# Four-layer convolution net on one core: where layer 1's first kernel is finished, relative to the first input transform

## The chip, the cores and the metric

The kernel runs on one core of a Trainium2 chip. The metric is device time in microseconds (us), median of several runs; smaller is better. Engines are called by the profile's names: PE (TensorE, matmul), PEld (its weight loads), DVE (VectorE), ACT (ScalarE), POOL (GpSimd), SP (SyncE, which issues most DMAs; ACT issues the others). A name such as L296 is line 296 of the kernel before.

## The reference

The input is `x` of 3 images, 256 channels, 48 by 48 pixels, in float32. Four residual layers follow each other:

```
x = x + L0(_gn(x))   # 1x1 conv + two rounds of attention and MLP + 1x1 conv over the concatenation
x = x + L1(_gn(x))   # per-image 3x3 convolution, kernel mixed from 8 experts
x = x + L2(_gn(x))   # one 3x3 convolution with bias
x = x + L3(_gn(x))   # a state-space scan over the pixels
```

`_gn` is a group normalisation over 32 groups of channels. Layer 1 is where the change lies:

```
pooled  = x.mean(axis=(2, 3))
routing = sigmoid(pooled @ routing_ws)                 # one weight per image and expert
ws      = einsum('ne,eoihw->noihw', routing, weight)   # a 3x3 kernel of its own for each image
y       = 3x3 convolution of image n with ws[n], padding 1
```

So no convolution of an image can begin before its own kernel has been mixed: 8 experts of 256 x 256 x 9 weights, each times that image's weight.

## The kernel before

**The end of layer 0.** The images are taken in `ORDER = (2, 1, 0)`; the loop variable `n` counts 0, 1, 2 and `b` is the image. For each image the last MLP runs over six chunks ("strips") `c` of 384 columns: `hidden` (L518 matmuls, L523 gelu on ACT), then `add_back` of the strip before (L529 matmuls, L533 on DVE). Then the concatenating 1x1 convolution runs over the same six strips: `concatenated` (L1031 matmuls, L1036 SiLU on ACT, L1041 the residual addition on POOL). `take_stats` (L1045, DVE) collects the statistics of the strip before. The strips' operands `yc` and `xc` are loaded on ACT's DMA queue (L1020, L1022).

**What is slipped in beside it.** After each strip `aside` is called. It takes one step of a short generator (`small_steps`) and then a given number of steps of the generator `mixing`, which is `mixed(2, upools[0])`: the kernel of image 2.

- `routing(b)` is the short generator for the weights of an image: group statistics (L183 to L192, with matmuls L186 and L195 and the power on POOL L164), scale and shift, `pooled`, and then the product. For each of the two channel halves, DVE spreads `pooled` over a 128x128 tile `pbc` (L373, one buffer), and PE multiplies it with the routing weights (L374). ACT takes the sigmoid (L378). It is stepped during the MLP of the next image; image 0 has no next one and its routing is run at once after the loop.
- `mixed` makes 48 steps, 8 experts times 6 pieces: each loads 384 KB from HBM on SP (L251, tile `wconv`, six buffers) and scales or adds it into the tile `u` (first expert on ACT, L294; the other 42 on DVE, L296). After those come two steps with a `kernel_transform` each, for one half of the input channels: six DVE operations on 128x768 (L258 to L263) that turn the three taps of a row into six Winograd points in `u`. These use `wconv` buffers for their intermediate sums.

**The first input transform.** At `b == 0 and c == 3` the kernel calls `input_transform(2, 0, ...)`: POOL zeroes the edges of `xpad` (L322, L325), ACT writes the normalised half image of image 2 (L331), and twelve DVE operations on 128x624 (L345 to L356) form six Winograd points in the tile `vt`. The third of them (L347) writes point 1, the fourth (L348) point 3. `xpad` has one buffer, `vt` two.

**Order.** From the mark before this loop up to the end of `mixing`, `keep_order` chains the instructions of PE, DVE, ACT and POOL in the order written. It doesn't chain SP's loads. What comes later, image 0's routing and all of layer 1, is placed by the framework's planner, which may put it between chained instructions.

**Layer 1.** Units go over images 2, 1, 0, two halves each, two output halves `m` each. `products` makes one Winograd point in six matmuls (L1589), in the order 1, 3, 4, 5, 0, 2; the sums go to DVE (L1607 to L1619). Beside unit 0 (image 2) the kernel of image 1 is mixed, beside unit 1 that of image 0, each with its transforms; one piece of the mixture in six is summed on PE (L282). From unit 2 on nothing is mixed any more.

Of the kernel before, what the change touches and what calls it, by code (L numbers as in the profile page):

```python
# [84 lines left out]
def net(  # L85
# [29 lines left out]
    def late_pool(name, bufs=1, stack=late_pools):  # L115
        return stack.enter_context(tc.tile_pool(name=name, bufs=bufs, side="right"))
# [93 lines left out]
    def group_norm_steps(b, psum, tag, stats=None, known=None):  # L210

        mv, gm, rstd = yield from norm_steps(
            [xs[b][:, ct, :] for ct in range(CT)], gmat, psum, tag, stats, known
        )
        sc = small.tile([P, CT], F32, name="gsc", bufs=4)
        nc.vector.tensor_copy(sc, rstd)
        sh = small.tile([P, CT], F32, name="gsh", bufs=4)
        nc.vector.scalar_tensor_tensor(sh, gm, -1.0, rstd, ALU.mult, ALU.mult)
        return mv, sc, sh
# [22 lines left out]
    def sixth(sc, sh):  # L242

        t = small.tile([P, 2, CT], F32, name="six", bufs=4)
        nc.vector.tensor_scalar(t[:, 0, :], sc, 1.0 / 6.0, None, ALU.mult)
        nc.vector.tensor_scalar(t[:, 1, :], sh, 1.0 / 6.0, None, ALU.mult)
        return t[:, 0, :], t[:, 1, :]
# [111 lines left out]
    def routing(b, psum, tag, stats):  # L359

        mv, sc, sh = yield from group_norm_steps(b, psum, tag, stats)
        norms[b] = sixth(sc, sh)
        pooled = small.tile([P, CT], F32, name="pooled")
        nc.vector.tensor_tensor(pooled, mv[:, :, 0], sc, ALU.mult)
        nc.vector.tensor_tensor(pooled, pooled, sh, ALU.add)
        yield
        pr = psum.tile([P, 512], F32, tag=tag, name="ps_r")  # L370
        for ct in range(CT):
            pbc = small.tile([P, P], F32, name="pbc", bufs=1)
            nc.vector.tensor_scalar(pbc, ones, pooled[:, ct : ct + 1], None, ALU.mult)  # L373
            nc.tensor.matmul(  # L374
                pr[:, :EXPERTS], pbc, rwt[:, ct, :], start=ct == 0, stop=ct == CT - 1
            )
        r = route[b] = const.tile([P, EXPERTS], F32, name=f"route{b}")
        nc.scalar.activation(r, pr[:, :EXPERTS], AF.Sigmoid)  # L378


    with ExitStack() as l0:
# [131 lines left out]
        def hidden(b, c):  # L513
            wf, fb = mlp[b]
            f = fpool.tile([P, 2, CH], F32, name="f")
            pf = pair()
            for m in range(2):
                nc.tensor.matmul(  # L518
                    pf[:, m, :CH], wf[:, m * P : (m + 1) * P], chunk(cur[b], c),
                    start=True, stop=True,  # L520
                )
            for m in range(2):
                nc.scalar.activation(f[:, m, :], pf[:, m, :CH], AF.Gelu, bias=fb[:, m : m + 1])  # L523
            return f

        def add_back(i, b, c, f):
            pf = psa.tile([P, 512], F32, name="acc")
            for m in range(2):
                nc.tensor.matmul(  # L529
                    pf[:, :CH], w("f2", (i * 2 + m) * P, P), f[:, m, :], start=m == 0, stop=m == 1  # L530
                )
            cc = chunk(cur[b], c)
            nc.vector.scalar_tensor_tensor(cc, pf[:, :CH], v("f2_b", i), cc, ALU.add, ALU.add)  # L533
# [483 lines left out]
        def parts(b, c):  # L1017

            yc = ypool.tile([P, 3, CH], F32, name="yc")
            nc.scalar.dma_start(yc, ycat[b][:, :, c * CH : (c + 1) * CH])  # L1020
            xc = ypool.tile([P, CT, CH], F32, name="xc")
            nc.scalar.dma_start(  # L1022
                xc, x[b, :, c * CH : (c + 1) * CH].rearrange("(t p) n -> p t n", p=P)
            )
            return yc, xc

        def concatenated(b, c, yc, xc):
            pz = pair()
            for m in range(2):
                for kt in range(4):  # L1030
                    nc.tensor.matmul(  # L1031
                        pz[:, m, :CH], w("cv2", kt * 256 + m * P, P),
                        yc[:, kt, :] if kt < 3 else chunk(cur[b], c), start=kt == 0, stop=kt == 3,
                    )
            for m in range(2):
                nc.scalar.activation(  # L1036
                    chunk(xs[b][:, m, :], c), pz[:, m, :CH], AF.Silu,
                    bias=b2sh[:, m : m + 1], scale=b2sc[:, m : m + 1],
                )
            both = xs[b][:, :, c * CH : (c + 1) * CH]  # L1040
            nc.gpsimd.tensor_tensor(both, both, xc, ALU.add)  # L1041

        def take_stats(b, c, stats):
            for m in range(2):
                nc.vector.bn_stats(stats[m][:, c, :], chunk(xs[b][:, m, :], c))  # L1045
# [8 lines left out]
        def aside(n):  # L1054

            if small_steps:
                try:
                    next(small_steps[0])
                except StopIteration:
                    del small_steps[0]  # L1060
            if 2 in route:
                for _ in range(n):
                    next(mixing, None)

        for n, b in enumerate(ORDER):
            held = None
            for c in range(NCH):
                f = hidden(b, c)
                if held is not None:
                    add_back(i, *held)  # L1070
                held = b, c, f
                aside(2)
            add_back(i, *held)
            stats = [
                small.tile([P, NCH, 6], F32, name=f"xst{m}", bufs=2) for m in range(CT)
            ]
            for c in range(NCH):
                concatenated(b, c, *ahead.pop(0))

                z = n * NCH + c + 2  # L1080
                if 3 <= z < len(chunks):
                    ahead.append(parts(*chunks[z]))
                if c:
                    take_stats(b, c - 1, stats)
                if b == 0 and c == 3:
                    vp = late_pool("vp", 2, last_pools)
                    pad = late_pool("pad", stack=last_pools)
                    first_v = input_transform(2, 0, *norms[2])
                aside(3)
            take_stats(b, NCH - 1, stats)  # L1090
            if b:
                curpools[b].close()
            small_steps.append(routing(b, psm, "m", stats))
# [485 lines left out]
    with ExitStack() as l1:  # L1579
# [117 lines left out]
        for n, (k, h) in enumerate(halves):  # L1697
            layer, b = units[k]
# [33 lines left out]
    with ExitStack() as l3:  # L1732
# [180 lines left out]
        for s, (at, m, h) in enumerate(steps):  # L1913
            if m == 0 and h == 1 and at + 2 <= last:
                fetch(at + 2)
            for part in range(8):
# [6 lines left out]
                if part == 0 and h == 0:  # L1923
                    c, n = (at, m + 1) if m + 1 < DI else (at + 1, 0)
# [69 lines left out]
def net_kernel(tc, *args):  # L1994

    with tc.tile_pool(name="flag", bufs=1) as pool:
        flag = pool.tile([1, 1], I32, name="flag")
        net(tc, *args, flag, False)
        bad = tc.nc.values_load(flag[:1, :1])
        with tc.If(bad > 0):  # L2000
            net(tc, *args, None, True)
# [77 lines left out]
```

## Time and profile before

| What | us |
|---|---|
| median of 3 runs | 3333.62 |
| lowest to highest of them | 3328.32 to 3335.85 |
| the profiled execution, device time | 3335.13 |
| its span in the profile | 3333.4 |
| PE busy | 3141.3 (94%) |
| DVE busy | 2862.1 (86%) |
| ACT busy | 2393.7 (72%) |
| POOL busy | 1334.0 (40%) |
| mean TensorE clock granted | 0.979 |

The span runs from the first to the last instruction of the profiled execution; 1.7 us lie around it. Times of places below are us from the span's start. Busy shares are averages over stages with different limits. The stage of the change lies at about 1440 to 1610 us, at the end of layer 0 and in the first unit of layer 1.

### The profile page before, as it was taken

Reading aid. Unit: us, or ns where it says so; the run is one execution under the profiler, and the core shown is the slowest. Engines: PE = TensorE matmul, PEld = TensorE weight load, DVE = VectorE, ACT = ScalarE, POOL = GpSimd, SP = SyncE. Lnnn points to the kernel's source line nnn. Section 1 sums busy time; section 2 is a strip of 40 time slices with the busy share of each in tenths; the row PEclk is TensorE's granted clock in tenths of the full one; section 3 lists DMA queues with packets and bytes.
Section 4 is the critical chain, followed back from the end, with each engine's and each line's share of the span. In section 5 each row is a group of like instructions: output and inputs, shape, how many; then the busy total and the mean of one; then the engine's idle time right before and its main releaser. Section 6 shows DMA issues by size and latency. Waiting matters only on the chain.

```text
span 3333.4 us, 54144 instructions
## 1 busy us (share of the span) xinstructions
PE 3141.3 (94%) x20890; PEld 1555.3 (47%) x20890; DVE 2862.1 (86%) x3234; ACT 2393.7 (72%) x3664; POOL 1334.0 (40%) x457
## 2 busy tenths in 40 slices
PE   7999999999999999988999997999999999999996
PEld 4334343353343434546777773444444444444442
DVE  3799989968988998369985448999999999999998
ACT  2688888838888887332323457888888888888884
POOL 0000000000000000120000007999999999999997
PEclk8999999999999999999999998999999999999997
DMA  4000000010000001475621025555555555455552
GB/s 167 32 8 10 8 8 7 8 47 5 8 7 8 10 8 44 162 248 200 204 75 41 34 65 138 133 128 131 135 135 141 134 139 135 122 134 139 146 131 56
DMA packets 182158, 290.76 MB, mean 87 GB/s; under 512 B 34737, under 2 KB 148465, under 8 KB 179970
## 3 DMA queue, kind: packets, MB, share of 16 engines
q1 hardware_dynamic: 168658, 267.15, 29.9%
q10 hardware_dynamic: 13232, 20.06, 1.8%
q8 instruction: 165, 2.70, 0.3%
q14 instruction: 103, 0.84, 0.1%
HBM read 236.24 MB, written 50.64 MB: 86 GB/s over the span
## 4 chain that ended last, share of the span: by engine, by line
PE 56%; DVE 29%; ACT 8%; issue 4%; DMA 3%; POOL 0%; SPq 0%; ACTq 0%; DVEq 0%; POOLq 0%
DVE hs L1860 20%; PE ps_s L638 16%; PE acc L651 14%; PE ps_c L1589 8%; DVE hs L1808 3%; ACT ps_da L1852 2%; PE ps_s L1031 2%; PE ps_y L462 2%; DVE u L296 2%; PE ps_m L665 2%; PE ps_m L711 1%; PE acc L529 1%; PE ps_s L518 1%; PE ps_g L1222 1%; DMA wconv<-in_we 1%
## 5 line engine op out<-in xcount | busy, mean ns | idle before, releaser
L642 ACT ACTIVATE pt<-ps_s 128x1024 f32<-128x1024 f32 x972 | 942.4, 1022 | 154.7 <-PE ps_s L638 142.1
L1860 DVE TENSOR_TENSOR_SCAN hs<-ps_da,hs 128x385 f32<-128x385 f32 x1152 | 1003.0, 940 | 5.8 <-ACT ps_da L1852 4.0
L857 DVE TENSOR_TENSOR part<-part,pt 128x2048 f32<-128x2048 f32 x396 | 906.8, 2290 | 41.2 <-ACT pt L642 18.4
L1852 ACT ACTIVATE ps_da<-dtr,u 128x384 f32<-128x384 f32 x1152 | 651.3, 580 | 119.9 <-DVE hs L1860 108.8
L164 POOL TENSOR_TENSOR rstd<-ve,mhalf 128x2 f32<-128x2 f32 (+1 forms) x26 | 16.3, 629 | 1475.1 <-DVE ve L162 1475.1
L638 PE MATMUL ps_s<-q,kt 32*128 32x512 f32 (+1 forms) x4320 | 576.3, 592 | 0.1
L651 PE MATMUL acc<-pt,vt 128*32 128x512 f32 (+1 forms) x4320 | 520.9, 561 | 0.2
L1589 PE MATMUL ps_c<-vt,u 128*128 128x288 f32 x1728 | 432.0, 411 | 21.6 <-DVE u L263 21.6
L1877 POOL TENSOR_TENSOR hc<-hs,x 128x3072 f32<-128x3072 f32 x72 | 405.3, 5629 | 11.5 <-DVE hs L1860 7.1
L1877 POOL TENSOR_TENSOR hc<-hs,bc 128x3072 f32<-128x3072 f32 x71 | 400.3, 5638 | 9.7 <-DVE hs L1860 5.5
L1589 PEld LDWEIGHTS ps_c<-vt,u 128*128 128x128 f32 x1728 | 330.4, 192 | 118.2 <-issue 20.4
L638 PEld LDWEIGHTS ps_s<-q,kt 32*128 32x128 f32 x4320 | 195.2, 183 | 199.1 <-issue 120.2
L651 PEld LDWEIGHTS acc<-pt,vt 128*32 128x32 f32 x4320 | 94.4, 108 | 353.4 <-issue 326.7
L1894 PE MATMUL ps_y<-hc,u 128*32 128x384 f32 x2304 | 227.3, 515 | 1.1 <-POOL hc L1877 1.1
L1273 PE MATMUL ps_g<-u 128*128 128x384 f32 x576 | 195.0, 491 | 23.3 <-ACT u L1269 23.3
L1826 POOL TENSOR_TENSOR hs<-dtur,x 128x1536 f32<-128x1536 f32 x72 | 209.2, 2905 | 7.3 <-DMA dtur<-dtud 7.3
L1826 POOL TENSOR_TENSOR hs<-dtur,bc 128x1536 f32<-128x1536 f32 x72 | 209.7, 2912 | 0.0
L1273 PEld LDWEIGHTS ps_g<-u 128*128 128x128 f32 x576 | 108.3, 190 | 106.9 <-ACT u L1269 34.5
L1605 ACT COPY cb<-ps_c 128x288 f32<-128x288 f32 x48 | 19.1, 398 | 155.8 <-PE ps_c L1589 141.4
L322 POOL MEMSET xpad<- 128x212 f32 x12 | 5.7, 471 | 308.2 <-ACT xpad L1640 229.1
L1894 PEld LDWEIGHTS ps_y<-hc,u 128*32 128x32 f32 x2304 | 62.1, 112 | 142.4 <-issue 129.6
L1392 PE MATMUL ps_g<-u 128*128 128x384 f32 x288 | 109.2, 513 | 13.0 <-ACT sz L1400 7.7
(275 smaller groups left out, 4137.7 us busy)
## 6 DMA issues: line engine op xcount, KB each, us to landing
wconv<-in_we SPq DMA_DIRECT2D x144, 384.0 KB, 4.2
dtr<-dtd SPq DMA_DIRECT2D x288, 192.0 KB, 3.7
dtur<-dtud SPq DMA_DIRECT2D x288, 96.0 KB, 4.2
wconv<-xd SPq DMA_DIRECT2D x36, 384.0 KB, 3.7
x<-bcd SPq DMA_DIRECT2D x72, 192.0 KB, 4.9
dtd<-x SPq DMA_DIRECT2D x36, 384.0 KB, 3.0
dtuq<-dtud SPq DMA_DIRECT2D x288, 48.0 KB, 2.0
bc<-bcd SPq DMA_DIRECT2D x72, 192.0 KB, 4.8
```

The source lines that it names most:

```text
L638: nc.tensor.matmul(s[:, j, cols], kt[r, mt * P : (mt + 1) * P], q[r, :n], start=True, stop=True,)
L642: nc.scalar.activation(p[:, h0 : h0 + 2, :], s, AF.Exp)
L651: nc.tensor.matmul(acc[h * HD : (h + 1) * HD, :n], vt[:, mt, g * P + h * HD : g * P + (h + 1) * HD], p[:, h, cols], start=mt == 0, stop=mt ...
L857: ): nc.vector.tensor_tensor(part, first, p, ALU.add)
L1273: nc.tensor.matmul(bank[m % 2], w3v["taps"][:, m, tap, :], w3v["xi"][:, m % 3, tap : tap + CH], start=tap == 0, stop=tap == DCONV - 1,)
L1392: nc.tensor.matmul(bank[j], w("in", ct * 512 + m * P, P), k.xn[:, ct, DCONV - 1 :], start=ct == 0, stop=ct == CT - 1,)
L1589: nc.tensor.matmul(pc[:, :HN], u[:, i, dy, ct, m * P : (m + 1) * P], vt[:, i, ct, dy * TW : dy * TW + HN], start=ct == 0 and dy == 0, stop ...
L1826: nc.gpsimd.tensor_tensor(states(s)[:, :, 2:4, 1:], chunks[at].rows[m][1].unsqueeze(1).broadcast_to([P, 2, 2, CH]), b_rows(s, 0, 2), ALU.mult,
L1852: nc.scalar.activation(slots[n % 3][:, 1 : CH + 1], chunks[at].rows[m][0][:, q, :], AF.Exp, scale=amat[:, col : col + 1],)
L1860: nc.vector.tensor_tensor_scan(b, slots[(8 * s + part) % 3][:, : CH + 1], b, 0.0, ALU.mult, ALU.add)
L1877: nc.gpsimd.tensor_tensor(hc, tiles[s][:, :, :, 1:], cb.broadcast_to([P, 2, 4, CH]), ALU.mult)
L1894: nc.tensor.matmul(k.y_ps[32 * q : 32 * q + 32, :CH], fold, hc[:, g, q, :], start=False, stop=h == 1 and g == 1,)
```

## The change

Two edits, both in the end of layer 0.

- `routing` gets one more `yield` for images 1 and 0, between the spreading of `pooled` on DVE and the product on PE, in each of the two channel halves. Run step by step (image 1), the first product is then issued one strip after its operand, and the second another strip later, together with the sigmoid. Run at once (image 0), nothing changes. Image 2 is left as it was.
- `aside` is given other counts while image 0 is worked on. In the MLP's strips 1, 3 and 5, three mixing steps are taken where two were. From strip 2 of the concatenation on the count is 99, so that in strip 2 all that is left of the generator is issued: the last three mixing steps and both kernel transforms. The first input transform, issued in strip 3, thus comes after them in the written order; before, the last three mixing steps came just after it and the kernel transforms one strip later.

```diff
@@ def routing(b, psum, tag, stats):
         for ct in range(CT):
             pbc = small.tile([P, P], F32, name="pbc", bufs=1)
             nc.vector.tensor_scalar(pbc, ones, pooled[:, ct : ct + 1], None, ALU.mult)
+            if b < 2:
+                yield
             nc.tensor.matmul(
                 pr[:, :EXPERTS], pbc, rwt[:, ct, :], start=ct == 0, stop=ct == CT - 1
             )
@@ for n, b in enumerate(ORDER):   # the MLP's strips
                 held = b, c, f
-                aside(2)
+                aside(3 if n == 2 and c % 2 else 2)
             add_back(i, *held)
@@                                 # the concatenation's strips
                 if b == 0 and c == 3:
                     vp = late_pool("vp", 2, last_pools)
                     pad = late_pool("pad", stack=last_pools)
                     first_v = input_transform(2, 0, *norms[2])
-                aside(3)
+                aside(3 if n < 2 or c < 2 else 99)
             take_stats(b, NCH - 1, stats)
```

## The prediction

> **What bounds the kernel now.** I read the page's chain of waits first: it goes over DVE and PE by turns, and in the stretch from 1440 to 1690 us mostly over DVE. Then the table of busy time by stretches (us; busy PE, PEld, DVE, ACT, POOL; PE clock, DMA share, GB/s):
>
> ```profile
> 1447.70:1452.70 5.00, 1.07 (x5) 0.98 (x5) 4.06 (x12) 1.16 (x1) 0.18 (x1) 0.83 0.71 231
> 1452.70:1458.00 5.30, 5.30 (x10) 2.92 (x11) 1.33 (x2) 2.51 (x4) 0.00 (x0) 0.52 0.55 181
> ...
> 1494.30:1512.90 18.60, 0.01 (x1) 0.04 (x1) 18.50 (x23) 8.22 (x10) 2.92 (x4) 0.62 0.20 63
> 1512.90:1533.60 20.70, 20.70 (x82) 15.06 (x82) 20.00 (x47) 5.74 (x7) 1.54 (x4) 0.93 0.39 135
> 1533.60:1605.60 72.00, 69.19 (x269) 51.59 (x269) 67.85 (x107) 17.82 (x31) 0.69 (x3) 0.98 0.68 230
> ```
>
> PE stands still from 1494.3 to 1512.9, while DVE is full. Afterwards both are nearly full until image 1's kernel is ready at 1605.6: DVE misses 0.7 + 4.2 us, PE 2.8. So two engines bound unit 0 together, and time is won only if both come earlier. What DVE waited for, first from 1440 to 1494.3, then to 1605.6:
>
> ```profile
> DVE xst L1045 <- POOL x L1041: 10.8, 4, 3.8
> DVE wc L345 <- ACT xpad L331: 5.4, 1, 5.4
> DVE cur L533 <- PE acc L529: 4.1, 1, 4.1
> DVE gsc L216 <- POOL rstd L164: 0.9, 1, 0.9
> DVE pbc L373 <- PE ps_r L374: 0.7, 1, 0.7
> ```
>
> ```profile
> DVE u L296 <- DMA wconv<-in_we: 3.8, 5, 1.4
> DVE gsc L216 <- POOL rstd L164: 0.6, 1, 0.6
> ```
>
> DVE waits 21.9 us ahead of its full stretch and then 4.4. The timeline of DVE shows what PE waits for (start, us, instruction, idle before):
>
> ```profile
> 1482.01 1.02 DVE L1045 BATCH_NORM_STATS2 xst<-x 128x6 f32<-128x384 f32 x2 [2.45 <-POOL x L1041]
> 1488.39 0.81 DVE L345 SCALAR_TENSOR_TENSOR wc<-xpad 128x624 f32<-128x624 f32 x1 [5.36 <-ACT xpad L331]
> ...
> 1490.68 2.42 DVE L348 TENSOR_TENSOR vt<-wc,we 128x624 f32<-128x624 f32 x1
> ...
> 1500.87 2.87 DVE L296 SCALAR_TENSOR_TENSOR u<-wconv,route,u 128x768 f32<-128x768 f32 x3
> ...
> 1511.79 0.95 DVE L263 TENSOR_TENSOR u<-wconv,u 128x768 f32<-128x768 f32 x1
> ```
>
> and the timeline of PE its two stalls:
>
> ```profile
> 1451.25 0.60 PE L374 MATMUL ps_r<-rwt,pbc 128*128 128x8 f32 x2 [3.55 <-DVE pbc L373]
> ...
> 1512.89 11.17 PE L1589 MATMUL ps_c<-vt,u 128*128 128x288 f32 x38 [18.59 <-DVE u L263]
> ```
>
> DVE idles for the padded image, transforms it, and only then mixes and transforms the kernel.
>
> **What the Trainium skill says.** "TensorE: Matmul & The Clock Gate" (What's actually happening) says that about 3.4 us of idleness puts the array on half its clock. Here the 3.55 us stall is followed by 5.3 us at 0.52; waits of 1.2 to 2.2 us in image 1's concatenation (1400 to 1436) left it at 1.00, but 0.9 + 0.4 us at 1391 was followed by 0.61. So a short stall may or may not cost clock. "ScalarE: Activation LUTs" (What ACT_TABLE_LOAD costs) gives 1283 ns for a table load; the trace has 1.28. "SBUF — State Buffer" (SBUF: two separate sides) says that a DVE operation with two SBUF inputs and a POOL operation that reads SBUF lock each other out: the one that starts first keeps the port, the other waits. The trace agrees: L348 and L353, begun just after a POOL addition, took 2.42 and 2.41 us instead of 0.80, and an addition begun during L296 took 2.14 instead of 1.81.
>
> **Edit 1, the product a strip later, with three mixing steps drawn into the MLP.** Before, PE ends `add_back` of strip 2 at 1447.7 and `add_back` of strip 5 at 1461.8. In those 14.1 us it has 2 x 1.35 (L518) + 3 x 1.3 (L529) = 6.6 us of work at full clock; 7.5 is lost, to the stall (3.5 + 0.4), the half clock (5.3 / 2 = 2.6), and the rest between. After it, DVE goes: strip 0 as now, to 1444.5; three steps for two in strip 1, +0.93, so `pooled` is ready about 1449.5; two steps, L533, and the first `pbc` at 1452.2, 0.9 later than now. But PE asks for it a strip later, after `hidden` 4 and `add_back` 3 at 1450.4: a stall of 1.8 us. Three steps (2.8), L533 and the second `pbc` end at 1455.7; PE is there at 1455.4. With `add_back` 5 PE ends at 1457.5 at full clock, 4.3 earlier; if the stall costs clock, 2.5. **I take 3.5, bounds 2.5 and 4.3.** Gelu of strip 4 is no longer behind the sigmoid, and one reload of gelu's table (1.28) goes; it is within the 4.3. Behind the waiting L374 stand `hidden` and `add_back` of the next strip, and DVE's L533 after those; that stall of DVE (4.1) falls to 0 to 1. DVE ends this part, with three more steps done, at 1461.5 instead of 1463.6.
>
> **SP and DMA.** The three steps bring three loads of 384 KB forward. At 302 GB/s (mean of 1464 to 1488) that is 3.9 us, and a pause at 1457 to 1461 is there for them. After that, the buffers of the last steps come free at about 1475 rather than 1504: four loads for image 1's kernel (1.57 MB, 5.2 us) then go beside `yc` and `xc` of strips 4 and 5 on the same 16 engines. Between nothing and 5.2 us more for strip 5's end at 1491; I take 1. If the pause were not there, the cost is 3.9 us on the concatenation.
>
> **Edit 2, kernel before input.** In strips 0 to 2 of the concatenation nine mixing steps are taken, as now. New in strip 2 are the twelve operations of the kernel transforms: 12 x 0.87 (start to start on DVE's timeline) = 10.5 us. POOL's additions of strips 2 and 3, which now fall into DVE's waits, fall among them: at 1.6 us a lock-out 0 to 3.2; I take 2.4, for the trace shows that a busy DVE does lose the port. Now the steps of strip 2 begin at 1476.7, after the statistics of strip 1; 3.5 earlier is 1473.2. Then 2.9 for the steps and 12.9 for the kernel: 1489.0. Statistics of strip 2, 0.9: 1489.9. ACT's `xpad`, now ready at 1488.3, is ready at 1485 and not waited for: the 5.4 go. The input transform (12.5 with two lock-outs, as now) runs from 1489.9 to 1502.4. PE's first product needs point 1, the third operation, at 1492.3, and a PSUM bank that ACT's last SiLU leaves (now 1495.6, then 1492). **PE starts at about 1493 instead of 1512.9.** It needs 2.9 us a point (12 matmul records of 0.245 each: PE's timeline has 64 in 15.68), and DVE delivers the other points by 1502.4.
>
> That lead of 20 us can't be kept, since DVE has to do the same work. After the input transform it has the statistics of strips 3 to 5 (2.8 us; POOL has long added them) and the second transform, whose `xpad` is written 2.2 us after the first one's end, behind those statistics. Eight of its operations (5.8) end at 1511.0. The same set ends now at 1522.6: **11.6 us** earlier. As a check, by waits: of 21.9 remain 2.8 (image 1's last strip, untouched), 0.9, some 2 and 2 for POOL in strips 0 and 1, and 0 to 1 for L533, together 7.7 to 8.7: 13.2 to 14.2 less 2.4 for the lock, so 10.8 to 11.8. I take 11.5; with the ends of every term 9 to 15.
>
> From there to 1690 DVE misses only 4.4 + 4 us, and its work is the same. PE is ahead, and image 0's routing also moves up with DVE. So image 1's kernel is ready 11.5 us earlier, unit 1 begins so much earlier and takes as long, and from unit 2 on everything follows PE, shifted. Sum: 3335.13 - 11.5 = 3323.6 for an execution like the profiled one, which was 1.5 above the median; against the median 3333.62 - 11.5 = **3322.1**.
>
> **Rivals.**
>
> - *DMA takes it back.* DVE's waits in unit 0 and 1 are all for `wconv`, loaded six buffers deep. 48 tiles at 1.2 to 1.3 us are about 60 us, against 92.7 of unit 0. If the waits grow from 4.4 to 10 us, since a buffer waits for an L282 stuck in PE's queue, 5.9 us remain: 3327.7. Against it: DMA share is 0.39 and 0.68 in unit 0, and loading begins earlier.
> - *PE gets more.* If PE's lead frees the L282 buffers earlier, the 3.8 us and part of the 4 of unit 1 go too: gain 16, 3317.6.
> - *Only edit 1 counts.* DVE is late again in unit 0 and edit 2 is a mere exchange: gain 3.5, 3330.1. The idle DVE in front of L345 speaks against it.
> - *Slower: routing of image 0 in PE's queue.* The planner places its five small products (now at 1523.9 to 1533.5, behind three points). DVE reaches their statistics at 1503 at the earliest, 1510 if the second transform goes first. Put ahead of nearly all points, they hold PE for their chain, 10 us now: PE would be free at 1520, 7 later than now. With PE's 2.8 us of slack until 1605.6 that is 4.3 slower, and with a spell of half clock (2.6, as above) 6.9; I take that end: 3340.5. It decides from 1515.7 on. Against it: now the planner puts 19 matmuls ahead of the first of them.
> - *The change is not what is executed*, if the planner put the second transform's or layer 1's operations among the kernel's: `xpad` has one buffer, so it can't; only 2 in 100, with no difference.
>
> **How the numbers follow.** About 0.2%, 6.7 us, is what a measurement of this kernel can tell from no change. Forecast (9 to 15) 0.56; more 0.13; DMA 0.12; only edit 1 0.09; slower 0.08; not executed 0.02. All of the first two, and half of DMA's, are over 0.2%: 0.75. Slower by over 0.2%: the planner's case, 0.08. Within: the rest, 0.17. The range leaves out the slower case and half of edit 1's alone: from 3315 (gain 18.6) to 3330.
>
> **What would show it.** Right: PE's gap at 1494 falls below 4 us; L345 no longer waits for `xpad`; the last L263 ends before the first L345; PE's stall before L374 is under 2 us; DVE's waits from the start of image 0's MLP fall to about 8 us; unit 2 begins some 11.5 us before 1688.4. Wrong: PE held at L186, L195 or L374 in unit 0, or DVE waiting over 8 us for `wconv` there, or a first product that waits for a bank or for `yc` past 1500.

## The result, and the profile after

The changed kernel takes 3324.28 us (median of 9 runs, 3323.07 to 3327.43) against 3334.62 us for the kernel before on the same chip: ratio 0.9969, 95% interval 0.9961 to 0.9978. That is 10.3 us faster, with 7.3 to 13.0 in the interval. Forecast were 11.5.

In the profiled executions the MLP of image 0 begins at 1436.84 us before and at 1438.85 us after. Nothing that was changed comes ahead of it, so everything below is counted from there. The table of busy time by stretches, cut at the same places in both kernels, gives the stage at a glance: the MLP, the concatenation, the gap in front of the first product, unit 0 to the end of image 1's kernel, unit 1 to the end of the first half of image 0's kernel. The columns are those of the prediction's table: start and end, length, busy time of PE, PEld, DVE, ACT and POOL (with the number of instructions), granted clock, DMA share and GB/s. First the kernel before, then the changed one:

```profile
1436.84:1461.76 24.92, 20.46 (x58) 11.33 (x57) 16.23 (x34) 12.71 (x19) 2.51 (x2) 0.86 0.69 226
1461.76:1494.30 32.54, 31.36 (x97) 17.96 (x95) 19.16 (x24) 8.86 (x13) 10.14 (x8) 1.00 0.72 246
1494.30:1512.89 18.59, 0.00 (x0) 0.03 (x1) 18.49 (x23) 8.22 (x10) 2.92 (x4) 0.62 0.20 63
1512.89:1605.90 93.01, 90.20 (x350) 66.91 (x351) 88.16 (x153) 23.86 (x38) 2.23 (x7) 0.97 0.62 208
1605.90:1688.39 82.49, 77.06 (x307) 57.55 (x306) 77.93 (x130) 22.07 (x35) 1.39 (x4) 0.99 0.67 230
```

```profile
1438.85:1459.65 20.80, 17.89 (x58) 9.52 (x57) 18.08 (x36) 10.88 (x18) 2.84 (x2) 1.00 0.83 282
1459.65:1498.30 38.65, 33.15 (x97) 18.66 (x95) 34.91 (x39) 9.41 (x13) 10.31 (x8) 0.96 0.77 251
1498.30:1499.67 1.37, 0.00 (x1) 0.03 (x1) 1.33 (x3) 1.23 (x2) 0.02 (x1) 1.00 0.00 0
1499.67:1598.54 98.87, 87.07 (x340) 64.29 (x341) 92.99 (x158) 33.62 (x50) 5.18 (x11) 0.96 0.57 193
1598.54:1680.40 81.86, 79.70 (x315) 60.04 (x313) 75.70 (x128) 13.97 (x23) 1.38 (x4) 0.99 0.64 214
```

The lengths are the second column: the MLP is 4.1 us shorter, the concatenation 6.1 longer, the gap 17.2 shorter, unit 0 5.9 longer, unit 1 0.6 shorter. Together 251.55 became 241.55: 10.0 us. The two profiled executions as a whole differ by 7.7 us, since the second one reached this MLP 2.0 us later; behind the stage both take 1645 us. DVE's busy time is the third after the length. In the concatenation it went from 19.2 to 34.9 us: the kernel's work lies there now, beside PE, where before DVE idled. DVE's waits from the MLP to the first product, in the list of waits, were 21.9 us; after:

```profile
DVE xst L1047 <- POOL x L1043: 5.1, 3, 1.7
DVE gsc L216 <- POOL rstd L164: 0.9, 1, 0.9
```

The timeline of PE has the stalls that are left (start, us, instruction, idle before it and what ended it; lines of the changed kernel lie two higher from L376 on):

```profile
1454.52 0.39 PE L376 MATMUL ps_r<-rwt,pbc 128*128 128x8 f32 x2 [1.89 <-DVE pbc L373]
...
1474.72 3.72 PE L1033 MATMUL ps_s<-yc,w0b 128*128 128x384 f32 x6 [4.59 <-DMA yc<-ycat]
...
1499.67 8.48 PE L1591 MATMUL ps_c<-vt,u 128*128 128x288 f32 x34 [1.37 <-ACT x L1038]
```

and the timeline of DVE the new order:

```profile
1483.07 2.57 DVE L258 SCALAR_TENSOR_TENSOR wconv<-u 128x768 f32<-128x768 f32 x1
...
1491.02 0.96 DVE L263 TENSOR_TENSOR u<-wconv,u 128x768 f32<-128x768 f32 x1
1491.89 1.01 DVE L1047 BATCH_NORM_STATS2 xst<-x 128x6 f32<-128x384 f32 x2
1492.82 0.79 DVE L345 SCALAR_TENSOR_TENSOR wc<-xpad 128x624 f32<-128x624 f32 x1
1493.53 2.41 DVE L346 SCALAR_TENSOR_TENSOR we<-xpad 128x624 f32<-128x624 f32 x1
```

The last L263 ends ahead of the first L345, and L345 waits for nothing. L258 and L346 took 2.57 and 2.41 us instead of 0.96 and 0.80: each began just after an addition of POOL (at 1483.02 and 1493.34), which held the port. L262 and L352 were held up in the same way (2.46 and 2.42 us), so there are four lock-outs where the kernel before had two. PE's concatenation took 6.1 us longer. Whether that mattered is told by the chain of waits across it (start, us, what):

```profile
1459.81 10.33 PE ps_s L1033 x32
...
1471.48 2.15 POOL x L1043
...
1474.59 2.86 DVE u L296 x3
1477.45 0.88 DVE wconv L258
...
1491.02 0.04 DVE u L263
```

The chain leaves PE at strip 1 (1470.1), goes over POOL's addition of that strip to DVE, and stays there. PE's 4.6 us wait for `yc` at 1474.7 is not on it.

### The profile page after: what moved, and what is told of

It reads as the page before. It is cut to its first block, busy times and chain, and to the rows that moved or that the text cites. A ratio compares the mean times of both kernels' runs of the same rounds, so it can differ in the third digit from the quotient of the medians.

```text
span 3325.7 us, 54145 instructions
## 1 busy us (share of the span) xinstructions
PE 3138.1 (94%) x20890; PEld 1551.0 (47%) x20890; DVE 2864.1 (86%) x3234; ACT 2391.5 (72%) x3663; POOL 1334.5 (40%) x457
## 4 chain that ended last, share of the span: by engine, by line
PE 55%; DVE 30%; ACT 8%; issue 4%; DMA 2%; POOL 0%; SPq 0%; DVEq 0%; ACTq 0%; POOLq 0%
DVE hs L1862 20%; PE ps_s L640 16%; PE acc L653 14%; PE ps_c L1591 8%; DVE hs L1810 3%; ACT ps_da L1854 2%; PE ps_s L1033 2%; PE ps_y L464 2%; PE ps_m L667 2%; PE ps_m L713 1%; DVE u L296 1%; PE acc L531 1%; PE ps_g L1224 1%; PE ps_s L520 1%; PE ps_y L1896 1%
## 5 line engine op out<-in xcount | busy, mean ns | idle before, releaser
L859 DVE TENSOR_TENSOR part<-part,pt 128x2048 f32<-128x2048 f32 x396 | 906.5, 2289 | 41.3 <-ACT pt L644 18.5
L1879 POOL TENSOR_TENSOR hc<-hs,x 128x3072 f32<-128x3072 f32 x72 | 405.2, 5628 | 12.6 <-DVE hs L1862 8.7
```

Source lines behind the costliest of these rows:

```text
L859: ): nc.vector.tensor_tensor(part, first, p, ALU.add)
L1879: nc.gpsimd.tensor_tensor(hc, tiles[s][:, :, :, 1:], cb.broadcast_to([P, 2, 4, CH]), ALU.mult)
```

## The experiments

Each was timed in five rounds against the kernel before. Gains are worked out as (1 - ratio) x 3335 us. The edits are against the changed kernel. Beside the gains stands the profile's stage, from the start of image 0's MLP to the end of the first half of image 0's kernel, with DVE's busy and idle time in it:

| Kernel | ratio, 95% interval | gain, us | stage, us | DVE busy, idle |
|---|---|---|---|---|
| before | | | 251.6 | 220.0, 31.6 |
| changed | 0.9969 (0.9961 to 0.9978) | 10.3 | 241.6 | 223.0, 18.5 |
| e1 | 0.9996 (0.9988 to 1.0004) | 1.3 | 247.3 | 218.8, 28.4 |
| e2 | 0.9980 (0.9972 to 0.9988) | 6.7 | 243.4 | 222.2, 21.2 |
| e3 | 0.9987 (0.9979 to 0.9996) | 4.3 | 246.3 | 220.2, 26.1 |
| e4 | 0.9966 (0.9954 to 0.9978) | 11.3 | 238.8 | 222.3, 16.5 |
| e5 | 0.9979 (0.9971 to 0.9986) | 7.0 | 244.7 | 227.4, 17.3 |
| e6 | 0.9984 (0.9977 to 0.9992) | 5.3 | 244.9 | 225.3, 19.6 |
| e7 | 0.9955 (0.9942 to 0.9969) | 15.0 | 238.8 | 219.6, 19.2 |
| e8 | 0.9949 (0.9935 to 0.9962) | 17.0 | 237.1 | 219.7, 17.4 |
| e9 | 0.9970 (0.9959 to 0.9981) | 10.0 | 242.2 | 220.6, 21.6 |
| e10 | 0.9989 (0.9980 to 0.9997) | 3.7 | 248.5 | 218.9, 29.6 |

An interval reaches 3 us to either side, and up to 4.5 for e4, e7, e8 and e9. So two of the kernels are told apart by the times only if their gains lie some 4 us apart, 5 to 6 where one of those four takes part. The stage of a single profile follows the gains within 3 us. In the twelve profiles image 0's MLP begins anywhere from 1430.9 to 1441.4 us, though no edit lies ahead of it, and what follows the stage takes 1642.9 to 1645.9: most of the scatter between executions lies ahead of the stage, and the stage leaves it out. How much the stage itself varies from one execution to the next was not measured.

**e1, the later product alone**

```diff
-                aside(3 if n == 2 and c % 2 else 2)
+                aside(2)
-                aside(3 if n < 2 or c < 2 else 99)
+                aside(3)
```

> Only the later product: the counts of mixing steps are as in the kernel before, so the kernel of image 2 is finished behind the first input transform. Theory (DVE's idle time decides): PE enters image 0's concatenation about 4 us earlier, and padded image, input transform and kernel follow it, so 3 to 4 us faster than before. Rival (DMA takes it back): the strips' loads can't come earlier, PE waits for yc instead, 0 to 1 us faster.

1.3 us, not told from none. This lies next to the rival's range, but the interval (-1.3 to 4.0) also holds the theory's 3 to 4, so the times don't decide. The MLP is even shorter than expected, 18.8 us instead of 24.9, since with two steps a strip `pbc` comes earlier. The concatenation is 35.5 instead of 32.5. The timeline of PE in e1:

```profile
1454.80 0.39 PE L376 MATMUL ps_r<-rwt,pbc 128*128 128x8 f32 x2 [0.96 <-DVE pbc L373]
1472.40 3.64 PE L1033 MATMUL ps_s<-yc,w0b 128*128 128x384 f32 x6 [2.70 <-DMA yc<-ycat]
```

Half of what the MLP saves goes into the wait for `yc` and the half clock behind it. The stage of this profile is still 4.3 shorter; its MLP began 3.5 us later than before, with image 1's concatenation longer, which is within the scatter of the starts.

**e2, the counts alone**

```diff
-            if b < 2:
-                yield
```

> Only the counts: image 2's kernel is finished in front of the first input transform, and image 1's routing product is issued in the strip of its operand, as before. Theory (DVE's idle time decides): PE's stall for pbc grows from 3.5 to about 4.5 us and DVE's wait for L533 returns, the other waits go: 6 to 8 us faster than before. Rival (DMA): PE's stall leaves DMA its pause, the wait for yc does not arise, and 9 to 10 us are won, nearly as much as with both edits.

6.7 us, in the theory's range. PE's stall for `pbc` is 4.48 us, and DVE's wait for L533 3.2. The rival fails in its cause as well: PE waited 3.7 us for `yc` here too, in two waits. So the counts alone bring most of what both edits bring.

**e3, the kernel just behind the input transform**

```diff
-                aside(3 if n < 2 or c < 2 else 99)
+                aside(3 if n < 2 or c < 3 else 99)
```

> As the changed kernel, but both kernel transforms are issued in strip 3, just behind the first input transform instead of a strip in front of it. Theory (DVE's idle time decides): DVE has nothing to do between the mixing steps of strip 2 and the padded image, some 7 us of waits come back (for POOL's addition and for xpad), so 2 to 5 us faster than before. Rival (the start of PE's first product decides, not DVE): the first product starts with the first half's kernel at about 1504, 9 us earlier than before, and 6 to 9 us are won.

4.3 us, as the theory had it. Both edits are in but for the order. The rival was not put to the test that was meant: it counted on a first product 9 us earlier, and the product came 4.5 us earlier, counted from the MLP, about as much as was gained. e5 below parts the two. The timeline of DVE in e3 has its waits back:

```profile
1482.20 1.02 DVE L1047 BATCH_NORM_STATS2 xst<-x 128x6 f32<-128x384 f32 x2 [6.71 <-POOL x L1043]
1488.29 0.81 DVE L345 SCALAR_TENSOR_TENSOR wc<-xpad 128x624 f32<-128x624 f32 x1 [5.07 <-ACT xpad L331]
```

Idle time is 26.1 instead of 18.5. Placing the kernel's work *into the waits* is what pays, some 6 us of the 10.3.

**e4, the changed kernel with the strips' loads one strip earlier**

```diff
+        spare = ExitStack()
+        extra = late_pool("extra", stack=spare)
-        def parts(b, c):
+        def parts(b, c, ypool=ypool):
...
+                if n == 2 and c == 0:
+                    ahead.append(parts(*chunks[14], extra))
...
-                z = n * NCH + c + 2
+                z = n * NCH + c + (3 if n == 2 else 2)
...
+                    spare.close()
                     vp = late_pool("vp", 2, last_pools)
```

> As the changed kernel, but from image 0 on yc and xc are asked for one strip earlier, with a buffer of their own for strip 2. Theory (DVE decides): the 4.6 us wait of PE for yc goes, PE's first product comes up to 3 us earlier, and the time stays as with the change, 9.5 to 11.5 us faster than before. Rival (PE's late end of the concatenation cost the difference to the forecast): 4 us more are won, 14 us faster than before.

11.3 us, in the theory's range, but the rival's 14 lies in the interval (7.3 to 15.3) too, so the times don't decide. The profile is that of the fastest of six executions. In it the wait for `yc` is gone and the concatenation takes 31.4 us instead of 38.7, but the stage is only 2.8 shorter than with the change alone: most of the rest turned into a wait for DVE. In the list of PE's waits in e4:

```profile
PE ps_c L1596 <- DVE vt L347: 7.4, 1, 7.4
```

**e5 and e6, more work on one engine in unit 0**

```diff
+    transforms = []
...
-        stt(c, d[2], -4.0, d[4], ALU.mult, ALU.add)
-        stt(e, d[1], -4.0, d[3], ALU.mult, ALU.add)
+        transforms.append((b, h))
+        for _ in range(5 if len(transforms) == 2 else 1):
+            stt(c, d[2], -4.0, d[4], ALU.mult, ALU.add)
+            stt(e, d[1], -4.0, d[3], ALU.mult, ALU.add)
```

> The changed kernel with 5.8 us more work on DVE: the first two operations of image 2's second input transform are done five times (8 x 0.72 us), with the same values. Theory (DVE sets the time of unit 0): all of it shows, and 4 to 6 us remain of the 10.3 that the change won. Rival (PE sets it): DVE has room, and 9 to 11 us faster than before is kept.

```diff
+            if at_unit == 0 and m == 0:
+                nc.tensor.matmul(
+                    pc[:, :HN], u[:, i, 0, 0, m * P : (m + 1) * P], vt[:, i, 0, :HN],
+                    start=True, stop=True,
+                )
```

> The changed kernel with 5.9 us more work on PE in unit 0: the first matmul of each of the 12 products with m equal to 0 is done twice (12 x 0.49 us), with the same values. Theory (DVE sets the time of unit 0): PE's wait of 6.2 us at the end of unit 0 for image 1's kernel takes it up, and 8 to 11 us faster than before is kept. Rival (PE sets it): it shows in full, and 4 to 5 us remain.

7.0 and 5.3 us. By the times alone the theory is missed in e6: PE's extra work cost 5.0 of its 5.9, more than DVE's, which cost 3.3 of its 5.8; that 3.3 is not told from none. The profiles say where. At the end of unit 0, when image 1's kernel is done, e5 is at 164.6 us from the MLP and e6 at 159.5; the changed kernel is at 159.7. So in these profiles 4.9 of DVE's 5.8 us show in unit 0 and nothing of PE's. The first product of e5 comes only 0.4 us later than in the changed kernel, counted from the MLP, so its start alone, the rival of e3, doesn't set the time. In unit 1, where neither kernel does anything more, e5 needs 80.0 us, e6 85.4, the changed kernel 81.9. In e6 the planner placed layer 1 otherwise: image 0's first input transform begins 38.3 us after image 1's second, in the changed kernel 25.5. That spacing alone does not make the loss: the kernel before, e1, e3, e9 and e10 have it too (36.7 to 37.4 us), and their unit 1 takes 81.3 to 82.9. What the 85.4 come from stays open, and with it which of the two engines bounds units 0 and 1 together.

**e7, three of POOL's additions on DVE**

```diff
-            nc.gpsimd.tensor_tensor(both, both, xc, ALU.add)
+            engine = nc.vector if b == 0 and c >= 3 else nc.gpsimd
+            engine.tensor_tensor(both, both, xc, ALU.add)
```

> The changed kernel, with the residual additions of image 0's strips 3 to 5 on DVE instead of POOL and the loads as they are. Theory (POOL's additions lock DVE out on DVE's own path): three lock-outs of 1.6 us go and three operations of 0.9 us come, 12 to 13 us faster than before. Rival (the gain seen with both together came from the earlier loads): 9.5 to 11 us faster, as with the change alone.

15.0 us, more than expected. Its interval, 10.3 to 19.3, holds the theory's 12 to 13 and also the rival's upper end. The timeline of DVE in e7 shows that the exchange took place:

```profile
1491.95 0.95 DVE L1044 TENSOR_TENSOR x<-x,xc 128x768 f32<-128x768 f32 x1
...
1494.46 0.80 DVE L346 SCALAR_TENSOR_TENSOR we<-xpad 128x624 f32<-128x624 f32 x1
```

An addition on DVE takes 0.95 us; L346 is back at 0.80. DVE's busy time in the stage falls by 3.4 us, though DVE does three additions more. The stage is 2.8 us shorter than with the change alone, while the first product comes only 0.9 us earlier.

**e8, e4 and e7 together**

The edits of both.

> The changed kernel with the strips' loads one strip earlier, and with the residual additions of image 0's strips 3 to 5 on DVE instead of POOL. Theory (DVE sets the time, and POOL's additions take its port): three lock-outs of 1.6 us go and three operations of 0.9 come, so 2 us more than with the earlier loads alone: 13 to 14 us faster than before. Rival (a lock-out only uses up time in which DVE would have waited): no gain over the earlier loads alone, 10 to 12 us faster than before.

17.0 us, above the theory's range, whose 13 to 14 lie within the interval (12.7 to 21.7); the rival's 10 to 12 do not. The median is 3320.89 us. By its ratio it is the fastest kernel here, though its interval overlaps those of e4 and e7 (median 3320.83 us, on another chip).

**e9, the later product with the earlier loads; e10, the earlier loads alone**

e9 is e1 with e4's edit; e10 is e9 without the `yield`, so the kernel before with e4's edit alone.

> Only the later product, with the counts of before, and the strips' loads of image 0 one strip earlier. Theory (the 4 us that the later product saves PE are lost again to the wait for yc, since these loads queue behind the mixture's): with the loads earlier 3 to 4 us faster than before. Rival (the later product saves nothing that lasts, whatever the loads do): 0 to 1.5 us faster.

> The kernel before with nothing but image 0's loads one strip earlier: no later product, no other counts. Theory (the later product and the earlier loads need each other: one shortens PE's MLP by 4 to 6 us, the other lets the concatenation keep it): only the 1.2 us wait for yc of the kernel before goes, 1 to 2 us faster. Rival (the earlier loads alone made the 10 us that were won with the later product): 8 to 10 us faster.

10.0 and 3.7 us. I had expected 3 to 4 for e9, and both its ranges are missed; for e10 the rival's 8 to 10 fall. In e9 the MLP takes 19.2 us instead of 24.9 and the concatenation 31.1 instead of 32.5, so the padded image is ready earlier and the first L345 starts 7.6 us earlier, counted from the MLP. The kernel before goes from concatenation to padded image, to input transform, to kernel transform, to first product, and what the front of this chain gains reaches the end of it. e10 keeps the long MLP and has the 1.4 us of the concatenation; the rest of its 3.7 is within its interval (1.0 to 6.7). So beside the earlier loads the later product is worth some 6 us, more than e1 shows. That the two need each other is not shown: alone they bring 1.3 and 3.7 us, 5.0 less than together, which is about what the intervals leave open, and by the profiles' stages it is 4.3 and 3.1 against 9.4. DVE's waits between the MLP and the first product in e9:

```profile
DVE xst L1049 <- POOL x L1045: 7.9, 4, 2.9
DVE wc L345 <- POOL xpad L325: 4.2, 1, 4.2
DVE gsc L216 <- POOL rstd L164: 0.9, 1, 0.9
```

13.0 us where the kernel before had 21.9. They shrank without any work moved into them; PE was through the MLP and the concatenation 7.2 us sooner. So filling DVE's waits is one way to this gain, and not the only one.

## Why the prediction was right

**The sum.** The forecast was DVE's idle time saved less the lock-outs added: 13.2 to 14.2 less 2.4. In the stage DVE's idle time fell from 31.6 to 18.5 us, 13.1, and its busy time rose from 220.0 to 223.0, by 3.0. That is 10.0 us of stage, and 10.3 by the medians. Busy and idle time always add up to the stage; what tests the prediction is where the idle time went. Ahead of the first product it fell by 15.7 us, from 22.2 to 6.5 (in the tables above, length less DVE's busy time), and DVE's listed waits to 6.0 where about 8 were forecast. In units 0 and 1 it rose from 9.4 to 12.0, where the prediction took it as unchanged. That these two misses nearly cancel is luck. That the filled waits are the cause is borne out by e2 and e3; e9 shows that the same gain can be had in another way.

**Edit 1.** 3.5 us were taken, with bounds of 2.5 and 4.3; the MLP got 4.1 shorter. PE's stalls are 1.89 and 0.44 us (1.8 and 0.3 were worked out), and the clock stayed at 1.00.

**SP and DMA: the mis-sized term.** I took 1 us and named 3.9 "if the pause were not there". The concatenation lost 6.1. SP issued six loads of 384 KB from 1458.9 to 1464.6, ahead of `yc` at 1465.1, and two more behind it by 1466.5. PE got its `yc` at 1474.7. In between SP's queue moved 1.63 MB; in the kernel before it moved 0.85 MB between the issue of that `yc` (1467.2) and its landing (1473.3). The Trainium skill, "DMA: Bandwidth & Descriptors" (Issuing engines are not separate DMA queues), says that DMAs of all issuing engines run on the same 16 engines; here `yc` on ACT's queue shared them with SP's loads, and while PE waited (1470.1 to 1474.7) they moved 360 GB/s, against 251 over the whole concatenation. The 6.1 us are the longer waits (5.5 instead of 1.2) and a half clock (six records in 3.72 us instead of 2.10). The missing pause is not the whole cause: PE also waited for `yc` in e1, without the extra steps (2.7 us), and in e2, with the stall for `pbc` left in (3.7). The forecast survived since that loss lay beside the chain of waits; the profile of e4 agrees, where 7.2 us of concatenation came back and only 2.8 of the stage. It was no part of the argument that it would be, so here too the forecast had luck.

**Edit 2.** Kernel transforms, 12.9 expected: 14.6, of which 3.1 lock-outs (0 to 3.2) and the rest a start-to-start time of 0.96 on the mean instead of 0.87. Input transform, 12.5: 12.6. `xpad` is not waited for, as worked out.

**The first product.** It was to come 20 us earlier and came 13.2 earlier, 15.2 counted from the MLP. It waited for the bank that the last SiLU leaves, because of the late concatenation, until 1499.67; one of the prediction's signs of being wrong was such a wait past 1500. As said, this lead could not be kept: PE's idle time in unit 0 rose from 2.8 to 11.8 us.

**The rivals.** "DMA takes it back" was right on PE and wrong on the place: not in unit 0's waits for `wconv` (4.4 us against 3.8), but in the concatenation. "PE gets more" falls: its 16 us lie outside the interval, and the waits for `wconv` did not shrink. "Only edit 1 counts" falls with e2, where edit 2 alone brings 6.7 us (4.0 to 9.3). "Slower" didn't come: the planner put 17 matmuls ahead of L186, and PE waited 1.1 and 0.6 us on image 0's routing. That the change was not executed falls by DVE's timeline.

**What the prediction didn't see.** It took the later product alone as worth 3.5 us; beside the earlier loads it brings some 6 (e9 less e10). And it said that PE has slack in unit 0; the profiles of e5 and e6 bear that out up to the end of unit 0, and leave open why PE's extra work costs 5 us in the end.

## What to carry to other kernels

Before moving work, add up what the engine it runs on waits for ahead of its full stretch, and work out how much of it the work can fill: that part, less the port conflicts that the filled waits will meet, came close to the gain here (13.1 less 3.0 us over the stage). When an engine gets ahead, look at what it will ask for next: here PE waited 4.6 us for a load that shared the DMA engines with eight others, and where the loads were asked for one strip earlier (e4, e9) the wait was gone. If two engines share a port and one of them is short of time, a short operation can be cheaper on that engine itself (0.95 us) than on the other (a 1.6 us lock-out); in e7 this took 3.4 us off DVE's busy time, while the time won over the changed kernel, 4.7 us, is within the noise of the two.

## What the runs showed of the hardware that I had not expected

POOL's addition blocks DVE's SCALAR_TENSOR_TENSOR too: 2.57 us for 0.96 and 2.41 for 0.80, where in the kernel before only two TENSOR_TENSOR operations of DVE were held up (L348 and L353). The half clock came after shorter stalls than the 3.55 us of the kernel before, and the length of one stall does not tell whether it comes: in e1 2.70 us (up to 1472.40) were followed by 3.6 us at 0.59, and 2.03 us (up to 1433.45) by 3.0 us at 0.66, but 2.72 us (up to 1426.03) left it at 1.00, as did 1.89 us in the changed kernel.
